# A mixture-of-experts layer pair on one core: conditional blocks between its phases replaced by one at the end, with 23 instead of 24 quads of expert tiles

## The chip, the cores and the metric

One core of a Trainium2 chip. The metric is device time in microseconds (us) of one execution; the figure for a kernel is the median of its runs.

## The reference

4,096 tokens (16 sequences of 256) of width 128 go through half an expert layer, attention, and half an expert layer again, with the same expert weights both times:

```
x = x + 0.5 * ffn(layernorm(x))
x = x + attention(layernorm(x))
x = x + 0.5 * ffn(layernorm(x))

ffn(x): t = rmsnorm(x) * norm_scale;  g = t @ gate_w.T + gate_b          # 32 experts
        vals, idx = top_k(g, 4);      w = softmax(vals)
        out = sum over the 4 experts e of w_e * (w2_e @ swiglu(w1_e @ t + b1_e) + b2_e)
        return x + out
```

Attention is linear (queries and keys are softmaxed over the width, scores are divided by their sum), 16 heads of 8. All is float32.

## The kernel before

**Tiles.** Tokens come in blocks of 512 (four subtiles of 128) and groups of four blocks; there are two groups, 0 and 1. For each group and each of the two expert layers the kernel sorts token rows by expert: in each subtile an expert's rows are rounded up to units of RB = 5, an expert's units of the whole group to tiles of BT = 25 units (125 rows of width 128). A tile belongs to one expert. Four tiles make a quad. At most NT = 112 tiles (NQ = 28 quads) can be needed, whatever the routing; how many are needed is known only on the chip.

**Phases.** `experts(st, lo, hi, beside)` (line 684) runs the quads of one group in one layer. Four such phases follow one another: first layer of group 0 and 1, last layer of group 0 and 1. Here they are called f0, f1, l0 and l1. Each runs NQS = 24 quads. In a phase, `enter(q)` loads a quad's rows from DRAM (`xq`, two DMAs on SyncE's queue, L696), lets GpSimd copy the four tiles' first weights out of `w_sb` at an address read from a table (L703), and transposes the rows on TensorE (`pxT`, L709); `first(q)` is the first matmul (`ph`, 16 instructions, L723) with its activation on ScalarE (L727) and VectorE (L728, L733); `second(q)` is the second (`po`, 8 instructions, L741), the copy out of PSUM on ScalarE (`yq`, L746) and two stores to DRAM (`ys`, L748, SyncE).

**Beside it.** After each quad `beside()` takes a few steps of another chain of work, so that TensorE has both in its queue. Beside f0 goes `enter(1)`: norm, gate and top-4 of group 1 (`route`, L437) and its sorting (`dispatch`, L519), whose end is 16 scatters of rows (`xs`, L589, GpSimd's queue; the five `p` matmuls at L665 and the copies at L669 and L670 make the rows). Beside f1 goes `middle(0)`: it gathers the results of f0 (`gt<-ys`, L784), combines them (`pa`, `pwb`, L796 to L798, then `pu`, L814 and L817), does the attention of group 0, routes its last layer and scatters. Beside l0 goes `middle(1)`, beside l1 `leave(0)` (gathers, combines, stores the output); `leave(1)` stands alone at the end. `finish()` emits what is left of a chain. So l0 needs the scatters of `middle(0)`, f1 those of `enter(1)`, l1 those of `middle(1)`; and a gather needs all stores of its phase.

**Missing tiles.** `dispatch` also writes `over`, the number of experts that end before tile NQS*NJ; it is 32 if the first NQS quads hold all tiles (L584). After f0, and again after l0, `others` takes the smaller `over` of the two groups (L763), loads it into a register of every engine (`values_load`, L764), and puts the quads 24 to 27 of both groups into a conditional block (L768), so that the program is cut there: every engine branches. On the way that leaves the quads out, each engine's semaphores are set to what the quads would have made them, and SyncE does so only after the DMAs before it have landed. At the start, zeros are written to the rows of `ys` that the first NQS quads do not write (L266).

**Order.** Each engine works through its own queue in order. The order is set when the program is built, out of the order in the code and the dependencies; within one block, instructions of different phases can be interleaved, across a block's edge they cannot.

Of the kernel before, what the change touches and what calls it, by code (L numbers as in the profile page):

```python
# [13 lines left out]
I32 = mybir.dt.int32  # L14
AF = mybir.ActivationFunctionType
ALU = mybir.AluOpType
# [6 lines left out]
P = 128  # L23
# [3 lines left out]
GB = 4  # L27
GJ = GB * NJ
NE = 32
# [13 lines left out]
NT = (GJ * P + NE * (BT - 1)) // BT  # L43
NT = -(-NT // NJ) * NJ
NQ = NT // NJ
NQS = 24
NB = NT * BT
LIMIT = 7.0
ALPHA = 1.702
# [7 lines left out]
def kernel(  # L57
# [22 lines left out]
    nc = tc.nc  # L80
    n_tok = x.shape[0]
    n_blk = n_tok // TB
    n_grp = n_blk // GB
# [9 lines left out]
    small = ctx.enter_context(tc.tile_pool(name="small", bufs=2))  # L93
# [8 lines left out]
    x_tiles = {}  # L102

    def load_x(b):
        xt = tmp.tile([P, NJ, P], F32, tag="rows", name=f"x_{b}", bufs=8)
        nc.sync.dma_start(xt.rearrange("p (i s) h -> p i (s h)", i=SEQ), x_blk[b])
        x_tiles[b] = xt
# [153 lines left out]
    for g in range(n_grp):  # L261
        rest = ys[g][NQS * NJ * BT :, :].rearrange("n w -> (n w)").rearrange(
            "(p c w) -> p c w", p=P, c=4
# [69 lines left out]
    def moments(srcs, name):  # L333

        n = len(srcs) * NJ
        bufs = 2 if len(srcs) == 1 else 1
        stats = small.tile(
            [P, n, nc.vector.BN_STATS_DIM], F32, tag=f"stats{n}", name=f"st_{name}", bufs=bufs
        )
        mv = small.tile(  # L340
            [P, n, nc.vector.BN_AGGR_DIM], F32, tag=f"mv{n}", name=f"mv_{name}", bufs=bufs
        )
        for j in range(n):
            nc.vector.bn_stats(stats[:, j, :], srcs[j // NJ][:, j % NJ, :])
            nc.vector.bn_aggr(mv[:, j, :], stats[:, j, :])
        return mv

    def inverse_root(v, y, t):

        nc.vector.tensor_scalar(  # L350
            t.bitcast(I32), v.bitcast(I32), 1, None, ALU.logical_shift_right
        )
        nc.vector.tensor_scalar(
            y.bitcast(I32), t.bitcast(I32), -1.0, float(0x5F3759DF), ALU.mult, ALU.add
        )
        for _ in range(3):
            nc.vector.scalar_tensor_tensor(t, y, -0.5, v, ALU.mult, ALU.mult)
            nc.vector.tensor_tensor(t, t, y, ALU.mult)
            nc.vector.scalar_tensor_tensor(y, t, 1.5, y, ALU.add, ALU.mult)
        return y  # L360

    def coefficients(srcs, name):

        mv = moments(srcs, name)
        mean, var = mv[:, :, 0], mv[:, :, 1]
        n = len(srcs) * NJ
        bufs = 2 if len(srcs) == 1 else 1

        def new(tag, k):
            return small.tile([P, k, n], F32, tag=f"{tag}{n}", name=f"{tag}_{name}", bufs=bufs)  # L370


        rr, it, co = new("rr", 2), new("it", 2), new("co", 4)
        ra = it[:, 0, :]
        nc.vector.tensor_scalar(rr[:, 0, :], var, EPS, None, ALU.add)
        nc.vector.reciprocal(ra, rr[:, 0, :])
        nc.vector.tensor_tensor(ra, ra, var, ALU.mult)
        nc.vector.tensor_scalar(rr[:, 1, :], ra, EPS, None, ALU.add)
        rr = inverse_root(rr, new("iy", 2), it)

        nc.vector.tensor_tensor(co[:, 0, :], rr[:, 0, :], rr[:, 1, :], ALU.mult)
        nc.vector.scalar_tensor_tensor(
            co[:, 1, :], co[:, 0, :], -1.0, mean, ALU.mult, ALU.mult
        )
        nc.vector.tensor_scalar(co[:, 2, :], rr[:, 0, :], 0.5, 1.0, ALU.mult, ALU.add)
        nc.vector.scalar_tensor_tensor(
            co[:, 3, :], rr[:, 0, :], -0.5, mean, ALU.mult, ALU.mult
        )
        return co
# [4 lines left out]
    class Group:  # L394
# [12 lines left out]
        def enter(self, b):  # L407
            self.blocks.append(Block())
            self.held(b, "tn", [P, NJ, P], F32, GB + 1)
            self.blocks[b].xr = dram.tile(  # L410
                [P, NJ * P], F32, tag=f"xr_{self.name}{b}", name=f"xr_{self.name}{b}"
            )

            self.held(b, "rank", [P, P], BF16, 2 * GB + 2)
            self.held(b, "combT", [P, P], F32, 2 * GB + 2)
            return self.blocks[b]
# [102 lines left out]
    def dispatch(st, clear=False):  # L519
# [63 lines left out]
        st.over = grp.tile([P, 1], F32, tag="over", name=f"over_{name}", bufs=4)  # L583
        nc.vector.tensor_copy(st.over, pex[:, NQS * NJ : NQS * NJ + 1])  # L584
        yield
# [98 lines left out]
    def experts(st, lo, hi, beside):  # L684
# [51 lines left out]
        def second(q):  # L736
# [10 lines left out]
            for rows in parts:  # L747
                nc.sync.dma_start(ys_q[q].rearrange("j m h -> m j h")[rows], yq[rows])  # L748

        enter(lo)  # L750
        for q in range(lo, hi + 1):
            if q + 1 < hi:
                enter(q + 1)
            if q < hi:
                first(q)
            if q > lo:
                second(q - 1)
            beside()

    def others(a, b):  # L760

        over = small.tile([P, 1], I32, tag="over", name=f"over_{a.name}{b.name}", bufs=1)
        nc.vector.tensor_tensor(over, a.over, b.over, ALU.min)  # L763
        taken = nc.values_load(  # L764
            over[0:1, 0:1], min_val=0, max_val=NE,
            skip_runtime_bounds_check_because="made on the chip, a count of experts",
        )
        with tc.If(taken < NE):  # L768
            for st in (a, b):
                experts(st, NQS, NQ, lambda: None)  # L770

    def combined(st, b, tag):

        name = f"{st.name}{b}"
# [149 lines left out]
    waiting = deque()  # L924

    def step(n=1):
        for _ in range(n):
            while waiting:
                try:
                    next(waiting[0])  # L930
                    break
                except StopIteration:
                    waiting.popleft()

    def finish():
        while waiting:
            step()

    first = [Group(g, f"f{g}") for g in range(n_grp)]
    last = {}  # L940

    def staggered(chains, gap, most=2):

        chains = deque(chains)
        going = deque()
        while chains or going:
            if chains and len(going) < most and (not going or going[-1][1] >= gap):
                going.append([chains.popleft(), 0])
            for c in list(going):
                try:  # L950
                    next(c[0])
                    c[1] += 1
                    yield
                except StopIteration:
                    going.remove(c)

    def routes(g, gap, most):
        srcs = []
        for b in range(GB):
            if g > 0:  # L960
                load_x(g * GB + b)
            srcs.append(x_tiles.pop(g * GB + b))
        co = coefficients(srcs, f"f{g}")
        yield

        def block(b):
            yield from route(first[g], srcs[b], b, co[:, :, b * NJ : (b + 1) * NJ])

        yield from staggered((block(b) for b in range(GB)), gap, most)

    def enter(g):
        yield from routes(g, 2, 2)
        yield from dispatch(first[g], True)

    def middle(g):
        last[g] = Group(g, f"l{g}")

        def block(b):
            for x1 in combined(first[g], b, "x1"):
                yield  # L980
            for x2 in attention(x1, f"{g}{b}"):
                yield
            yield from route(last[g], x2, b, coefficients([x2], f"l{g}{b}"))

        yield from staggered((block(b) for b in range(GB)), 12)
        yield from dispatch(last[g])

    def leave(g):
        def block(b):
            for y in combined(last[g], b, "x1"):  # L990
                yield
            nc.sync.dma_start(
                out_blk[g * GB + b], y.rearrange("p (i s) h -> p i (s h)", i=SEQ)
            )
            yield

        yield from staggered((block(b) for b in range(GB)), 3)
# [10 lines left out]
    b1_rows = dram.tile([NE, 2 * P], F32, tag="b1_rows", name="b1_rows")  # L1008
    nc.scalar.dma_start(b1_rows, b1_t)

    waiting.append(routes(0, 1, GB))
    for c in range(NE // 2):
        step(2)
# [27 lines left out]
    banks.clear()  # L1041
    banks.append((ps_bg, "bg"))
    fold_attention()
    beside = [enter(1), middle(0), middle(1), leave(0)]
    steps = [3, 6, 6, 2]
    for i in range(2 * n_grp):
        waiting.append(beside[i])
        experts(first[i] if i < n_grp else last[i - n_grp], 0, NQS, lambda: step(steps[i]))
        finish()
        if i % 2 == 0:  # L1050
            others(*((first if i == 0 else last)[g] for g in range(n_grp)))
    waiting.append(leave(1))
    finish()


# [59 lines left out]
```

## Time and profile before

| | |
|---|---|
| median of 3 runs | 747.09 us (746.89 to 747.17) |
| the profiled execution | 768.92 us |
| its span, first to last instruction | 767.2 us |
| mean granted TensorE clock | 0.922 |
| HBM | 58.80 MB read, 64.04 MB written |
| first TensorE work of f0, f1, l0, l1 | 87.19, 217.09, 405.78, 619.60 us |
| last work before the output's last store is issued | 763.82 us |

The profile was taken in an execution of its own, longer than the runs; sums over its rows are made against its own time. Its span is cut into rows by engine. A group line reads: source line, engine, operation, output<-inputs, shape, count | busy us, mean ns of one | idle us of the engine just before them, and what ended most of it. PE is TensorE's matmuls, PEld its weight loads, DVE VectorE, ACT ScalarE, POOL GpSimd, SP SyncE; a "q" behind an engine's name is its sequencer or its DMA queue. Names that end in `_f` or `_l` belong to the first or the last layer. In a timeline, the number in brackets is the idle time before an instruction and what ended it.

### The profile page before, as it was taken

What the parts mean: (1) busy time and instruction counts of PE and PEld (TensorE: products, weight loads), DVE (VectorE), ACT (ScalarE), POOL (GpSimd) and SP (SyncE); (2) the same over time, 40 slices, a digit from 0 to 9 for tenths busy, and PEclk for the clock granted to TensorE, in tenths of its full rate; (3) what the DMA queues carried; (4) which work ended last, traced back from release to release, by engine and by line L of the source; (5) the groups of instructions that cost most, each with busy time, mean ns of one, the idle gap of its engine ahead of it and who ended that gap; (6) DMA issues with size and microseconds to landing.
All of it is one profiled execution on the core that took longest, in us unless ns stands there. A gap on an engine that the chain in (4) does not pass through costs nothing. (4 is left out here: it accounts for less than half of the span.)

```text
span 767.2 us, 16355 instructions
## 1 busy us (share of the span) xinstructions
PE 646.2 (84%) x4995; PEld 602.6 (79%) x5009; DVE 489.8 (64%) x1833; ACT 385.8 (50%) x918; POOL 291.2 (38%) x583
## 2 busy tenths in 40 slices
PE   3877598879969998897987889888889769999776
PEld 1567588879868888896886889878878659999776
DVE  6864777755527988965763587678767436654534
ACT  2843498445517458465452547464665414545410
POOL 3024433676363432121464231321226265543152
PEclk9978799999979999997998988898989979999989
DMA  7997355665565635223446342522435466766464
GB/s 235 369 334 280 124 148 163 216 234 188 144 165 137 175 84 149 55 83 108 168 168 187 112 144 69 139 79 68 107 111 184 155 157 196 222 170 176 118 185 157
DMA packets 136924, 123.98 MB, mean 162 GB/s; under 512 B 9858, under 2 KB 123970, under 8 KB 136834
## 3 DMA queue, kind: packets, MB, share of 16 engines
q1 hardware_dynamic: 121890, 73.16, 33.8%
q0 software_dynamic: 10960, 44.90, 17.5%
q10 hardware_dynamic: 3984, 4.82, 1.8%
q8 instruction: 45, 0.74, 0.4%
q14 instruction: 45, 0.37, 0.1%
HBM read 58.80 MB, written 64.04 MB: 160 GB/s over the span
## 5 line engine op out<-in xcount | busy, mean ns | idle before, releaser
L703 POOL COPY w_l<-w_sb 128x256 f32 x192 | 72.5, 407 | 144.5 <-PE ph_l L723 124.4
L703 POOL COPY w_f<-w_sb 128x256 f32 x192 | 74.0, 417 | 121.7 <-PE ph_f L723 108.3
L723 PE MATMUL ph_f<-xT_f,w_f 128*128 128x125 f32 x768 | 104.7, 285 | 2.9 <-DVE lin_f L728 1.6
L723 PE MATMUL ph_l<-xT_l,w_l 128*128 128x125 f32 x768 | 102.5, 284 | 0.0
L723 PEld LDWEIGHTS ph_f<-xT_f,w_f 128*128 128x128 f32 x768 | 98.0, 201 | 4.8 <-POOL w_f L703 2.7
L723 PEld LDWEIGHTS ph_l<-xT_l,w_l 128*128 128x128 f32 x768 | 96.6, 200 | 1.0 <-issue 0.9
L728 DVE TENSOR_SCALAR lin_f<-ph_f 128x250 f32<-128x250 f32 x96 | 39.3, 413 | 56.5 <-ACT a_f L727 46.5
L728 DVE TENSOR_SCALAR lin_l<-ph_l 128x250 f32<-128x250 f32 x96 | 39.4, 413 | 56.1 <-ACT a_l L727 55.5
L665 PE MATMUL p_f<-tn_f,o_f 128*128 128x128 f32 x320 | 47.1, 310 | 14.6 <-ACT s_f L669 6.5
L665 PEld LDWEIGHTS p_f<-tn_f,o_f 128*128 128x128 f32 x320 | 44.3, 221 | 16.9 <-ACT s_f L669 7.2
L741 PE MATMUL po_l<-w_sb,a_l 128*125 x384 | 55.3, 288 | 2.5 <-DVE a_l L733 1.7
L741 PE MATMUL po_f<-w_sb,a_f 128*125 x384 | 53.9, 283 | 3.1 <-ACT yq_f L746 1.3
L741 PEld LDWEIGHTS po_l<-w_sb,a_l 128*125 128x125 f32 x384 | 49.8, 200 | 4.2 <-ACT yq_l L746 2.1
L727 ACT ACTIVATE a_f<-ph_f 128x250 f32<-128x250 f32 x96 | 36.3, 384 | 33.3 <-PE ph_f L723 23.2
L727 ACT ACTIVATE a_l<-ph_l 128x250 f32<-128x250 f32 x96 | 36.0, 380 | 33.7 <-PE ph_l L723 27.1
L814 PE MATMUL pu_f<-gt_f,u_f 128*128 128x128 f32 x320 | 48.5, 295 | 5.0 <-DMA gt_f<-ys,row_f 4.5
L814 PE MATMUL pu_l<-gt_l,u_l 128*128 128x128 f32 x320 | 44.0, 283 | 9.0 <-DMA gt_l<-ys,row_l 7.7
L741 PEld LDWEIGHTS po_f<-w_sb,a_f 128*125 128x125 f32 x384 | 47.9, 194 | 4.6 <-ACT yq_f L746 2.6
L814 PEld LDWEIGHTS pu_l<-gt_l,u_l 128*128 128x128 f32 x320 | 40.8, 197 | 12.1 <-issue 8.5
L784 POOL DMA_INDIRECT gt_f<-ys,row_f x32 | 32.3, 1010 | 47.1 <-PE pu_f L814 25.6
L814 PEld LDWEIGHTS pu_f<-gt_f,u_f 128*128 128x128 f32 x320 | 43.8, 208 | 6.2 <-DMA gt_f<-ys,row_f 3.5
L589 POOL DMA_INDIRECT xs<-s_f,row_f x32 | 31.1, 972 | 44.7 <-ACT s_f L670 21.6
(338 smaller groups left out, 1464.0 us busy)
## 6 DMA issues: line engine op xcount, KB each, us to landing
xq_f<-xs SPq DMA_DIRECT2D x48, 224.0 KB
ys<-yq_f SPq DMA_DIRECT2D x48, 224.0 KB
xq_l<-xs SPq DMA_DIRECT2D x48, 224.0 KB
ys<-yq_l SPq DMA_DIRECT2D x48, 224.0 KB
xs<-zero SPq DMA_DIRECT2D x14, 500.0 KB
w_sb<-in_w_dram SPq DMA_DIRECT2D x4, 1024.0 KB
x<-in_x_dram SPq DMA_DIRECT2D x8, 256.0 KB
xr_f<-xr_f ACTq DMA_DIRECT2D x8, 256.0 KB
```

The lines of the kernel that those rows point to most:

```text
L589: ins = nc.gpsimd.indirect_dma_start(out=xs[st.g][:, :], out_offset=bass.IndirectOffsetOnAxis(ap=index, axis=0), in_=rows.rearrange("p r h ...
L665: nc.tensor.matmul(p0[:, r, :] if r < 4 else p1[:, 0:P], o[:, r, :], k.tn[:, t, :], start=True, stop=True,)
L703: nc.gpsimd.tensor_copy(w[:, s, :], w_flat[:, bass.ds(at[2 * c + s], 2 * P)])
L723: nc.tensor.matmul(ph[:, part, s, 0:RT], w_q[c][:, s, part * P : (part + 1) * P], x_q[:, 2 * c + s, :], start=True, stop=True,)
L727: nc.scalar.activation(a[:, ts, :], ph[:, 0, :, 0:RT], AF.Silu, scale=ALPHA)
L728: nc.vector.tensor_scalar(lin[:, ts, :], ph[:, 1, :, 0:RT], LIMIT + 1.0, 1.0 - LIMIT, ALU.min, ALU.max,)
L741: nc.tensor.matmul(po[:RT, t, :], hT[:, t, :], w_flat[:, bass.ds(at[t] + 2 * P, P)], start=True, stop=True,)
L784: nc.gpsimd.indirect_dma_start(out=gt.rearrange("p r h -> p (r h)"), out_offset=None, in_=ys[st.g][:, :], in_offset=bass.IndirectOffsetOnA ...
L814: nc.tensor.matmul(pu[:, t, :], u[:, r, s, :], got[t][:, r, :], start=(r == 0), stop=False)
```

## The change

NQS goes from 24 to 23, so that a phase covers 92 tiles instead of 96. `others` and its two conditional blocks are gone; the four phases stand in one block. The four phases and their side chains are put into a function `groups(nq, clear)`. After its first call, `over` of all four sorts is reduced to the smallest, loaded once, and one conditional block repeats everything from the input rows on with NQ = 28 quads per phase. `Group` objects are made when a chain begins, the input of group 0 is loaded again in the repetition, and tiles and DRAM buffers of the repetition get names of their own. The program grows from about 9,700 instructions to about 19,000, of which 9,926 stand in the conditional block; of these, 4,329 are TensorE's and 740 SyncE's. In the program before, a conditional block holds 195 of TensorE's, 57 of ScalarE's and 49 to 52 of SyncE's.

```diff
-NQS = 24
+NQS = 23
...
-    def others(a, b):
-
-        over = small.tile([P, 1], I32, tag="over", name=f"over_{a.name}{b.name}", bufs=1)
-        nc.vector.tensor_tensor(over, a.over, b.over, ALU.min)
-        taken = nc.values_load(
-            over[0:1, 0:1], min_val=0, max_val=NE,
-            skip_runtime_bounds_check_because="made on the chip, a count of experts",
-        )
-        with tc.If(taken < NE):
-            for st in (a, b):
-                experts(st, NQS, NQ, lambda: None)
...
-    first = [Group(g, f"f{g}") for g in range(n_grp)]
-    last = {}
+    first, last = {}, {}
+    run_name = ""
...
-            if g > 0:
+            if g * GB + b not in x_tiles:
                 load_x(g * GB + b)
...
-    def enter(g):
+    def enter(g, clear):
+        first[g] = Group(g, f"{run_name}f{g}")
         yield from routes(g, 2, 2)
-        yield from dispatch(first[g], True)
+        yield from dispatch(first[g], clear)
...
-    beside = [enter(1), middle(0), middle(1), leave(0)]
-    steps = [3, 6, 6, 2]
-    for i in range(2 * n_grp):
-        waiting.append(beside[i])
-        experts(first[i] if i < n_grp else last[i - n_grp], 0, NQS, lambda: step(steps[i]))
-        finish()
-        if i % 2 == 0:
-            others(*((first if i == 0 else last)[g] for g in range(n_grp)))
-    waiting.append(leave(1))
-    finish()
+
+    def groups(nq, clear):
+
+
+        beside = [enter(1, clear), middle(0), middle(1), leave(0)]
+        steps = [3, 6, 6, 2]
+        for i in range(2 * n_grp):
+            waiting.append(beside[i])
+            st = first[i] if i < n_grp else last[i - n_grp]
+            experts(st, 0, nq, lambda: step(steps[i]))
+            finish()
+        waiting.append(leave(1))
+        finish()
+
+    groups(NQS, True)
+
+    over = small.tile([P, 1], I32, tag="most", name="most", bufs=1)
+    for st in (first[1], *last.values()):
+        nc.vector.tensor_tensor(first[0].over, first[0].over, st.over, ALU.min)
+    nc.vector.tensor_copy(over, first[0].over)
+    taken = nc.values_load(
+        over[0:1, 0:1], min_val=0, max_val=NE,
+        skip_runtime_bounds_check_because="made on the chip, a count of experts",
+    )
+    with tc.If(taken < NE):
+        run_name = "r"
+        waiting.append(enter(0, False))
+        finish()
+        groups(NQ, False)
```

More of the change, by code (lines that the diff above doesn't have):

```diff
@@ L959, in routes @@
         for b in range(GB):
-            if g > 0:
+            if g * GB + b not in x_tiles:
                 load_x(g * GB + b)
             srcs.append(x_tiles.pop(g * GB + b))
-        co = coefficients(srcs, f"f{g}")
+        co = coefficients(srcs, first[g].name)
         yield
@@ L969, in routes @@
         yield from staggered((block(b) for b in range(GB)), gap, most)
-    def enter(g):
+    def enter(g, clear):
+        first[g] = Group(g, f"{run_name}f{g}")
         yield from routes(g, 2, 2)
-        yield from dispatch(first[g], True)
+        yield from dispatch(first[g], clear)
     def middle(g):
-        last[g] = Group(g, f"l{g}")
+        last[g] = Group(g, f"{run_name}l{g}")
         def block(b):
@@ L980, in block @@
                 yield
-            for x2 in attention(x1, f"{g}{b}"):
+            for x2 in attention(x1, f"{run_name}{g}{b}"):
                 yield
-            yield from route(last[g], x2, b, coefficients([x2], f"l{g}{b}"))
+            yield from route(last[g], x2, b, coefficients([x2], f"{last[g].name}{b}"))
         yield from staggered((block(b) for b in range(GB)), 12)
@@ L1009 @@
     nc.scalar.dma_start(b1_rows, b1_t)
+    first[0] = Group(0, "f0")
     waiting.append(routes(0, 1, GB))
```

## The prediction

> **What bounds it now.** I read the page, then windows by stage, then the timeline where phases meet (f0, f1, l0, l1 are the four phases).
>
> ```profile
> PE 646.2 (84%) x4995; PEld 602.6 (79%) x5009; DVE 489.8 (64%) x1833; ACT 385.8 (50%) x918; POOL 291.2 (38%) x583
> ...
> L703 POOL COPY w_f<-w_sb 128x256 f32 x192 | 74.0, 417 | 121.7 <-PE ph_f L723 108.3
> ```
>
> TensorE (PE) carries the kernel. 192 copies are 2 groups x 24 quads x 4 tiles, so the conditional blocks ran none of their quads. They cost time all the same. Windows before and across each change of phase (stretch, length, busy us of PE, PEld, DVE, ACT, POOL, granted clock, DMA share, GB/s):
>
> ```profile
> 195.00:205.00 10.00, 10.00 (x93) 10.00 (x93) 4.94 (x10) 5.77 (x13) 3.10 (x11) 1.00 0.53 143
> 205.00:227.00 22.00, 13.77 (x90) 12.35 (x90) 7.92 (x19) 5.02 (x10) 10.32 (x19) 0.77 0.55 143
> 396.00:406.00 10.00, 7.33 (x62) 6.82 (x61) 2.61 (x5) 4.10 (x10) 5.29 (x11) 1.00 0.58 196
> 406.00:424.00 18.00, 14.59 (x95) 13.66 (x95) 6.68 (x17) 3.97 (x9) 10.43 (x16) 0.81 0.66 189
> 612.00:628.00 16.00, 7.72 (x40) 6.47 (x39) 5.30 (x14) 3.08 (x7) 8.91 (x18) 0.68 0.64 162
> ```
>
> PE is full in f0's last quads, idle 8.2 us around the first block (205 to 227) and 8.3 around the second (612 to 628). Around f1 to l0, where no block stands, it idles 2.7 + 3.4 us: a part of each gap is the data, not the block. The first gap in the timeline (start, us):
>
> ```profile
> 208.54 1.11 PE L741 MATMUL po_f<-w_sb,a_f 128*125 x8 [0.85 <-DVE a_f L733]
> 209.92 1.02 PE L798 MATMUL pwb_f<-comb_f,seg_f 128*128 128x512 f32 x2
> 214.05 15.15 SPq L696 DMA_DIRECT2D xq_f<-xs  x10
> 214.69 1.00 POOL L784 DMA_INDIRECT gt_f<-ys,row_f  x1 [13.52 <-SPq L768]
> 217.09 1.06 PE L709 MATMUL pxT_f<-ident,xq_f 125*128 125x125 f32 x4 [6.15 <-DMA xq_f<-xs]
> 219.33 1.19 PE L814 MATMUL pu_f<-gt_f,u_f 128*128 128x128 f32 x4 [1.17 <-DMA gt_f<-ys,row_f]
> ```
>
> SP may not load f1's first rows before the block's exit (it waits there for the stores in flight), though f1's last scatter was issued at 191.1. The second gap, and the branch itself:
>
> ```profile
> 599.12 6.46 PE L665 MATMUL p_l<-tn_l,o_l 128*128 128x128 f32 x40 [2.39 <-DVE o_l L657]
> 607.14 1.08 POOL L589 DMA_INDIRECT xs<-s_l,row_l  x1 [0.80 <-DVE lin_l L728]
> 616.27 11.73 SPq L696 DMA_DIRECT2D xq_l<-xs  x10
> 619.60 1.07 PE L709 MATMUL pxT_l<-ident,xq_l 125*128 125x125 f32 x4 [6.97 <-DMA xq_l<-xs]
> ```
>
> ```profile
> L768 PEldq COMPARE_BRANCH  x2: 3462/3808/4153, 209.5 to 611.2; - x2
> L768 ACTq COMPARE_BRANCH  x2: 45/45/45, 212.1 to 613.2; - x2
> L768 SPq COMPARE_BRANCH  x2: 50/50/50, 212.7 to 615.0; - x2
> ```
>
> **Is the repetition taken?** The new test at the end repeats everything if any of four groups needs over 92 tiles. That is data. I routed the reference's own inputs with the reference's top-4, split each block into its four subtiles, rounded each expert's count up to 5 and its rows up to 25: 90 and 87 tiles in f0 and f1, 90 and 87 in l0 and l1. Two tiles of margin; a tie decided otherwise moves a row, not three tiles. So the repetition should not run, and I go on with that.
>
> **The change part by part** (against the profiled 768.92; minus is a gain).
>
> 1. The 24th quad in f0 and l1. The last quads there start every 3.09 us (pxT at 707.47, 710.56) with PE full: 16 ph, 8 po and 4 pxT matmuls back to back. Nothing else sets the pace, enter(1) and leave(0) being done. 2 x 3.09 = -6.2.
>
> 2. The first block. In the changed program's order PE goes from f0's last po straight to f1's pxT, whose rows SP now loads among f0's last quads. But ys still has to land before the first gather gt, and PE takes its queue in order: after pxT, pwb, pxT, 8 ph, 4 ph, pxT, 4 ph and half a po it meets pu. I count that as 6.6 us at the full clock from the last po's end (8 ph 0.9, 8 po 0.9, 4 pxT 0.43, pwb 1.3). The chain yq copy 0.6, stores 1.3 behind one load on SP, landing 2.5 (ys at the end of the chain of waits) and gather to pu 4.6 (214.69 to 219.33) is 9.2. So pu stalls 2.6 and starts at +9.2, where before it started at +9.7 (209.65 to 219.33). By then the new order has done 4.9 us more of work (2 pxT, 16 ph, half a po). 0.5 + 4.9 = -5.3. Behind pu in PE's queue stand f1's next quads, so these 2.6 are real.
> [...] Between 0 and 2.3 I take -1.0. Part 2: -6.3 (ends -3 and -9).
>
> 3. f1 to l0. No block goes, but a quad does. Before, PE's order is: the last 20 p_l, 2 ph, a quad's po, the 24th quad's 16 ph, two quads' po, then pxT_l at 405.78, 8.0 us after the last p_l (397.76). That wait is the scatter, its landing, and SP's load, so the removed quad lay under it; ahead of the last p_l the changed order has only 0.2 us less. What is late next is the load itself. Its second half now stands behind the two stores of the last yq on SP (0.45 us each): pxT_l at about +9.1. Against that, the last stores go 2.5 us earlier, the gathers too, and pu starts near +14.1 instead of +17.9 (415.70), with 2.2 us less of work behind it. 3.8 - 2.2 = 1.6, less about 1 for a longer slow-clock stretch: -0.6 (ends +2 and -3.1, the whole quad).
>
> 4. l0 to l1, block two. The last p_l ends at 605.58; pxT_l came 14.0 after it. Without the block the same path as in 3: +9.1. That is -4.9, and the quad is in it (it lies under the same path). POOL's w copies and gathers are no longer held (7.5 us, released by PE's branch), so nothing new is late. Ends -2.5 and -8.
>
> 5. More zeros. ys's tail grows from 16 to 20 tiles: 2 x 0.25 MB at the start. DMA is full there (356 GB/s in 50 to 60) and the scatters of f0 wait on landing (4.1 us before 65.58): 0.5 MB / 356 = +1.4 (ends 0 and +1.5).
>
> 6. The new ending. Four small DVE minima and a copy (0.15 each) hide under PE. Then every engine loads the value (0.43 to 1.04 at L764) and branches over the whole repeated program. [...] The rows agree by engine: ACT and SP jumped some 50 instructions in 0.05 us, PE 195 in 3.5 to 4.2. Now SP jumps 740, PE 4,329. By ACT's row the end costs about +0.8 (eight waits, another hop); by PE's, SP, which issues the last output at 764.2, arrives at 764.2 + 0.55 + 3.8 = 768.6, past the present end of 767.2, and leaves about 1.1 later: +2.5. I take the latter (ends +0.8 and +4.5).
>
> Sum: -6.2 - 6.3 - 0.6 - 4.9 + 1.4 + 2.5 = -14.1, to 754.8 in the profile. The unprofiled median is 747.09/768.92 = 0.972 of the profiled time: -13.7, so **733.4**.
>
> **Rivals.**
> - *Gain at the joins is mostly given back* (17%). PE's in-order queue meets pu and pxT_l as at f1 to l0, and the blocks only hid those waits. For: that join idles 6.1 us without any block. Against: f1's rows are ready from about 194. Then parts 2 and 4 give -2 each: -6.2 - 4 + 1.4 + 2.5 = -6.3, or 741.
> - *All of it* (16%). Short stalls keep the clock up, the zeros hide, the branch is cheap: -6.2 - 9 - 3.1 - 8 + 0.8 = -25.5, or 722.
> - *The repetition runs* (2%): one group with a 93rd tile decides it. The price is a second pass with 28 quads per phase, without the weight loading before 87: about 733 + 0.97 x (680 + 20 x 3.09) = 1,450. Slower by far; the tile counts speak against it.
> - *The end alone eats the gain* (2%): would need over 16 us in part 6, four times PE's longest branch.
>
> The sum's case has 63%. 0.2% is 1.5 us, about what a measurement can tell from none. Range 726 to 741: it takes in the sum with its ends, not added all on one side, and reaches the first rival; left out are the outer part of the second, and the repetition. The ends together would give 722 to 744. Faster 95%, same 1%, slower 4%.
>
> **What would show it.** 184 copies per w tile, none more. PE idle between f0's last po and f1's first pxT under 1 us, then a stall of 2 to 3 before the first pu, with a lower clock or not. pxT_l after the last p_l of about 9 us at both later joins. The f0 phase beginning 1 to 1.5 us later than 87.19. Long branches on all engines at the end, and 2 to 3 us from the last output's issue more than now. It is wrong if the joins wait for something not counted here (SP's order of loads and stores, above all), or if a phase's inner pace changes with the new order.

## The result, and the profile after

The changed kernel took **737.72 us** (median of 6 runs, 736.46 to 746.78), the kernel before beside it 747.92 (6 runs, 746.89 to 750.70): 0.9876 of the time, with a 95% interval of 0.9840 to 0.9912. The forecast was 733.4 with a range of 726 to 741; the interval allows a gain of 0.9% to 1.6%.

The 768.92 us of the profile that the prediction is built on was an unusually long execution. A second profile of the same kernel took 749.91 us (span 748.2), and the comparison below is made with that one. TensorE did its work in the same order in both; the first had a lower granted clock (0.922 against 0.936).

What to look at first is time by phase, not the two totals. Each row is a stretch from one phase's first `pxT` to the next one's: the start with the weight loading, f0, f1, l0, l1, and the rest. The columns are stretch, length, busy us of PE, PEld, DVE, ACT and POOL, granted clock, DMA share, GB/s. First the kernel before, in its second profile:

```profile
0.00:87.00 87.00, 53.59 (x308) 40.05 (x309) 58.97 (x307) 37.55 (x99) 26.95 (x70) 0.90 0.86 289
87.00:209.30 122.30, 109.14 (x948) 105.15 (x948) 81.91 (x264) 78.63 (x178) 61.24 (x125) 0.96 0.61 182
209.30:396.00 186.70, 166.54 (x1332) 158.06 (x1332) 134.76 (x542) 104.46 (x255) 71.17 (x140) 0.94 0.44 132
396.00:599.00 203.00, 171.95 (x1339) 160.64 (x1340) 144.32 (x565) 108.05 (x259) 69.45 (x130) 0.93 0.43 128
599.00:704.40 105.40, 103.06 (x877) 99.95 (x878) 51.56 (x109) 50.58 (x114) 47.16 (x104) 0.97 0.66 180
704.40:748.20 43.80, 30.79 (x208) 27.00 (x206) 18.36 (x47) 5.38 (x13) 15.12 (x16) 0.88 0.52 160
```

The same windows of the changed kernel:

```profile
0.00:87.70 87.70, 55.87 (x307) 41.60 (x307) 58.79 (x306) 37.62 (x99) 26.49 (x70) 0.88 0.88 292
87.70:202.90 115.20, 106.60 (x917) 103.32 (x918) 75.88 (x251) 75.94 (x172) 62.80 (x125) 0.96 0.61 185
202.90:398.40 195.50, 166.53 (x1314) 154.59 (x1313) 142.33 (x562) 106.51 (x256) 67.69 (x130) 0.96 0.43 128
398.40:585.90 187.50, 164.75 (x1308) 155.47 (x1308) 137.04 (x552) 103.30 (x252) 66.98 (x128) 0.93 0.45 133
585.90:688.20 102.30, 100.13 (x849) 97.29 (x850) 50.06 (x106) 48.82 (x110) 45.90 (x98) 0.97 0.64 180
688.20:734.70 46.50, 30.82 (x208) 27.04 (x206) 18.37 (x47) 5.38 (x13) 15.14 (x16) 0.87 0.50 153
```

The prediction's six parts can be put on the same stretches. Part 2's -6.3 is -7.4 in f0 (the wait before `pxT` goes) and +1.1 in f1 (the wait at `pu` and its clock). Part 3's -0.6 is +1.1 in f1 (`pxT_l` later) and -1.7 in l0.

| stretch | predicted | measured |
|---|---|---|
| start | +1.4 | +0.7 |
| f0 | -3.1 - 7.4 = -10.5 | -7.1 |
| f1 | +1.1 + 1.1 = +2.2 | **+8.8** |
| l0 | -1.7 - 4.9 = -6.6 | **-15.5** |
| l1 | -3.1 | -3.1 |
| rest | +2.5 | +2.7 |
| sum | -14.1 | -13.5 |

The sum agrees with these two profiles, but three stretches do not: f1 lost 6.6 us more than forecast, f0 gained 3.4 less, and l0 gained 8.9 more. A total that fits because errors cancel explains nothing yet. The two profiles also differ by more than the medians do (13.5 against 10.2 us): the changed kernel's was the quickest of its six runs, 736.46 us.

At the joins themselves the forecast can be read in the timeline (start and length in us, engine, line, operation, count, and in brackets the idle time before it and who ended it). From f0 to f1, first the kernel before in its second profile:

```profile
201.01 1.11 PE L741 MATMUL po_f<-w_sb,a_f 128*125 x8 [0.85 <-DVE a_f L733]
...
209.34 1.06 PE L709 MATMUL pxT_f<-ident,xq_f 125*128 125x125 f32 x4 [5.92 <-DMA xq_f<-xs]
211.66 1.19 PE L814 MATMUL pu_f<-gt_f,u_f 128*128 128x128 f32 x4 [1.26 <-DMA gt_f<-ys,row_f]
```

and the changed kernel:

```profile
202.88 0.59 PE L709 MATMUL pxT_f<-ident,xq_f 125*128 125x125 f32 x4
203.31 0.38 PE L784 MATMUL pa_f<-rank_cf,seg_b_f 128*128 128x512 bf16 x1
...
209.69 0.60 PE L741 MATMUL po_f<-w_sb,a_f 128*125 x4
212.62 1.38 PE L802 MATMUL pu_f<-gt_f,u_f 128*128 128x128 f32 x10 [2.33 <-DMA gt_f<-ys,row_f]
213.84 0.56 PE L805 MATMUL pu_f<-b_sb,comb_f 128*128 128x128 f32 x2
214.20 2.34 PE L802 MATMUL pu_f<-gt_f,u_f 128*128 128x128 f32 x10
```

PE goes from `po` to `pxT` without idling and stands 2.33 us at the first `pu` (forecast 2.6), which starts 9.6 us after f0's last `po` ends (forecast 9.2). The second ten `pu` behind that wait take 2.34 us (granted clock 0.50 from 213.9 to 217.3); at a granted clock of 1.00 ten take 1.28 (at 218.81). From l0 to l1:

```profile
571.18 5.02 PE L665 MATMUL p_l<-tn_l,o_l 128*128 128x128 f32 x40
...
585.88 1.06 PE L709 MATMUL pxT_l<-ident,xq_l 125*128 125x125 f32 x4 [5.35 <-DMA xq_l<-xs]
```

`pxT_l` comes 9.7 us after the last `p_l` (571.18 + 5.02) at this join, and 9.75 at f1 to l0; the forecast said 9.1 for both. Before, in the second profile, these were 13.3 and 8.8.

### The profile page after: what moved, and what is told of

It is laid out like the page before. It is cut to its first block, busy times and chain, and to the rows that moved or that the text cites. A ratio compares the mean times of both kernels' runs of the same rounds, so it can differ in the third digit from the quotient of the medians.

```text
span 734.7 us, 15957 instructions
## 1 busy us (share of the span) xinstructions
PE 624.7 (85%) x4897; PEld 579.3 (79%) x4897; DVE 482.5 (66%) x1823; ACT 377.6 (51%) x902; POOL 285.0 (39%) x567
## 5 line engine op out<-in xcount | busy, mean ns | idle before, releaser
L703 POOL COPY w_f<-w_sb 128x256 f32 x184 | 71.5, 420 | 129.4 <-PE ph_f L723 120.5
L703 POOL COPY w_l<-w_sb 128x256 f32 x184 | 68.7, 404 | 120.3 <-PE ph_l L723 108.7
L723 PE MATMUL ph_f<-xT_f,w_f 128*128 128x125 f32 x736 | 98.6, 282 | 1.5 <-DVE lin_f L728 1.3
L723 PE MATMUL ph_l<-xT_l,w_l 128*128 128x125 f32 x736 | 99.6, 286 | 0.2 <-DVE mv_a L838 0.2
L723 PEld LDWEIGHTS ph_l<-xT_l,w_l 128*128 128x128 f32 x736 | 93.9, 202 | 1.4 <-issue 1.3
L723 PEld LDWEIGHTS ph_f<-xT_f,w_f 128*128 128x128 f32 x736 | 91.8, 198 | 2.8 <-issue 2.1
L741 PE MATMUL po_l<-w_sb,a_l 128*125 x368 | 51.4, 282 | 2.8 <-ACT yq_l L746 1.0
L772 POOL DMA_INDIRECT gt_l<-ys,row_l x32 | 30.6, 957 | 50.5 <-PE pu_l L802 23.7
L741 PEld LDWEIGHTS po_l<-w_sb,a_l 128*125 128x125 f32 x368 | 45.9, 194 | 4.0 <-ACT yq_l L746 2.2
L802 PE MATMUL pu_f<-gt_f,u_f 128*128 128x128 f32 x320 | 45.8, 284 | 2.8 <-DMA gt_f<-ys,row_f 2.3
```

The lines of the kernel that those rows point to most:

```text
L703: nc.gpsimd.tensor_copy(w[:, s, :], w_flat[:, bass.ds(at[2 * c + s], 2 * P)])
L723: nc.tensor.matmul(ph[:, part, s, 0:RT], w_q[c][:, s, part * P : (part + 1) * P], x_q[:, 2 * c + s, :], start=True, stop=True,)
L741: nc.tensor.matmul(po[:RT, t, :], hT[:, t, :], w_flat[:, bass.ds(at[t] + 2 * P, P)], start=True, stop=True,)
L772: nc.gpsimd.indirect_dma_start(out=gt.rearrange("p r h -> p (r h)"), out_offset=None, in_=ys[st.g][:, :], in_offset=bass.IndirectOffsetOnA ...
L802: nc.tensor.matmul(pu[:, t, :], u[:, r, s, :], got[t][:, r, :], start=(r == 0), stop=False)
```

## Experiments

Each kernel ran beside the kernel before, whose medians in these comparisons were 749.2 to 751.9 us. All profiles are single executions. One program instruction can be two rows of a trace: block 0's 24 `pu` are 48 rows.

**How far apart are two executions?** The kernel before, unchanged, compared with itself.

> The kernel before, unchanged, for a second trace. The first trace took 768.92 us where its runs take about 748, and its phase l0 is 214 us long where the changed kernel's is 190. If the first trace was an odd execution, l0 is about 190 here too and the span near 746. If the change itself shortened l0, it is 214 again. Either way the ratio is 1.000.

749.98 us, ratio 1.0014 (0.9985 to 1.0042). Its 20 runs go from 742.74 to 754.78. So a median tells some 0.3%, a single profile much less. Three kernels below that share one order in f1 (the changed one, the one without the ending, the one with l0 by hand) have f1 at 195.5, 195.3 and 197.1 us, so differences of 2 us between single profiles say nothing. The first profile of the kernel before, with its lower clock, has l0 at 213.8 where the second has 203.0.

**Only fewer quads.**

```diff
-NQS = 24
+NQS = 23
```

> The kernel before with 23 quads, the two blocks kept: quads and zeros alone. My sum: the quads of f0 and l1 count (-6.2), those of f1 and l0 lie under the path from the last p matmuls to the next phase's rows (-0.6 and 0), zeros +1.4: about -5 us, 743, ratio 0.993. The rival that a quad is worth its 3.09 us of TensorE in every phase: -11 us, 737, ratio 0.985. If the blocks hide the quads: no change.

734.26 us, ratio 0.9833 (0.9782 to 0.9883): with both blocks still there, at least as fast as the whole change, and near the 737 of the rival that this expectation names. But not by its account: l1 lost 2.6 us in the profile, while l0 lost 14.7 (203.0 to 188.3), against a quad's 3.1.

**Only no blocks** (the tiles beyond 96 would be left out; there are none with these inputs).

```diff
-        if i % 2 == 0:
-            others(*((first if i == 0 else last)[g] for g in range(n_grp)))
```

> The kernel before with 24 quads and no conditional block anywhere (it leaves out the tiles past the 96th, of which there are none here). The blocks alone, without the new ending. My sum: -6.3 at f0 to f1 and -4.9 at l0 to l1, x 0.97 = -11, 737, ratio 0.985. The rival that the joins only change their wait: -2 each, 744, ratio 0.995.

753.67 us, ratio 1.0108 (1.0051 to 1.0165): **slower**. Yet f0 fell by 5.3 us (7.4 were foreseen for its join) and l0 by 5.0 (4.9 foreseen). f1 rose from 186.7 to 199.1.

**No ending** (the repetition for an overfull choice is left out).

```diff
-    with tc.If(taken < NE):
-        run_name = "r"
-        waiting.append(enter(0, False))
-        finish()
-        groups(NQ, False)
```

> The changed kernel without the conditional block at the end (it leaves out the repetition, which is not needed here). My sum: 2.5 us less than the changed kernel, with the span ending about 3.4 us after the last vector instruction instead of 6.2: ratio to before about 0.984. The rival that the branches hide under the last output's landing: the same time as the changed kernel, 0.9876.

736.77 us, ratio 0.9858 (0.9806 to 0.9910). From the last store's issue to the end it takes 3.3 us (728.0 to 731.3), in the changed kernel 6.2 (728.5 to 734.7), before 3.4: part 6 is +2.9, forecast +2.5. The medians, 0.95 us apart and taken in different comparisons, cannot show it. f1 is 195.3 and l0 187.4, so the ending has nothing to do with those.

By now the joins and the end are near the forecast, and what moves the time is the pace inside f1 and l0. There the build had written TensorE's queue in one of two orders. They differ in where the work beside the experts stands. In the **wide** order the four transposes of attention's normed input (`ph<-h`) stand in quad 5; in the **tight** one in quad 4. In both, block 0's 24 `pu`, whose result the norm reads, end in quad 2, so the tight order leaves the norm on VectorE less time: between the last of these `pu` and the first `ph` PE has some 4.9 us of other matmuls in the tight order and 6.5 in the wide one (from the changed kernel's f1, 220.3 to 225.2, and from f1 by hand below, 224.8 to 231.3). The theory: the order makes the pace. The rival: f1 is longer because nothing drains f0's stores and gathers ahead of it.

**A step taken ahead.** Three attempts to get the wide order by an edit of the schedule: in the changed kernel for i == 1, in the kernel before for i == 2, and without blocks with 24 quads for both.

```diff
         waiting.append(beside[i])
+        if i == 1:
+            step(1)
```

> The changed kernel, whole, with one step of the work beside it taken ahead of the expert tiles of f1 (and of no other phase). In the program's order the weights' product pwb of block 0's combine then stands before f1's first pxT, and its 24 pu stand together before the last of quad 1's ph; l0 is as in the changed kernel. Theory A (f1 lost 9 to 12 us because its queue on TensorE was written in another order: pwb between the first two pxT and the pu behind quad 1's ph): f1 falls from 195.5 to about 185 us and the time from 737 to about 727 us. Theory B (f1 is longer because the gathers and the writes of f0, which the block used to drain, now run into it, whatever the order): f1 stays at 194 to 196 us and the time at 737 us.

> The kernel before, with 24 quads and both blocks, and one step of the work beside it taken ahead of the expert tiles of l0 alone. In the program's order l0's pwb then stands before its first pxT and the pu stand together, as in the quick phases; f0, f1 and l1 are untouched. Theory A (order): l0 falls from 203 to about 190 us and the time by 10 to 14 us, to about 736 us, though no quad and no block is gone. Theory B (l0 became quick since a quad of its work or of the one before went): l0 stays at 203 us and the time at 748 us.

> The kernel before with 24 quads, without the two blocks (so the tiles of an overfull choice would be left out; there are none here), and with one step of the work beside it taken ahead of f1's and of l0's expert tiles. The same without that step took 753.7 us, 1.1% more than the kernel before, with 199 us in f1 and 198 in l0. Theory A (order): f1 falls to about 186 and l0 to about 186 us, the time to about 730 us: the joins' 10 us are then seen in the time. Theory B (joins without blocks leave the next phase slower by themselves): both stay within 3 us of 199 and 198 and the time at 750 us or more.

734.92 us (0.9814, 0.9782 to 0.9846), 742.11 (0.9904, 0.9871 to 0.9937) and 745.90 (0.9944, 0.9902 to 0.9986). The expected 727, 736 and 730 were missed: f1 stayed at 193.6 us in the first, l0 at 195.8 in the second, and the third had 195.6 and 194.4. The build had made a third order, with the 24 `pu` together, but the transposes still in quad 4. So setting `pwb` and `pu` ahead, which these expectations took for the mark, does not give the quick phase. It is not worth nothing either: the medians are 2.8, 7.4 and 7.8 us below those of the same kernels without the step (the first and the third pair ran in different comparisons). The first of the three, read alone, spoke for the rival.

**24 quads in the changed kernel.**

```diff
-NQS = 23
+NQS = 24
```

> The changed kernel with 24 quads of expert tiles per phase again, all else as it is. In the program's order f1 and l0 then both have pwb between the first two pxT and the pu behind quad 1's ph. Theory A (order): l0 loses what the changed kernel gained there, 10 to 12 us, beside 6 us for the two quads of f0 and l1: about 755 us, slower than the kernel before. Theory B (the quads alone, 3.1 us in f0 and in l1 each and something in l0): about 744 us.

755.10 us, ratio 1.0066 (1.0037 to 1.0094), as the theory said: l0 went to the tight order and to 200.7 us.

**The order by hand.** This parts the theory from the rival. The 751 matmuls and transposes of a phase are chained in a given order, and nothing else is edited; in the traces PE's order in the phase is then the one asked for. "Quads 0 to 13" is the stretch from the start of quad 0's `pxT` to the start of quad 13's.

```diff
+            n0 = len(nc.cur_bb.bb.instructions)
             experts(st, 0, nq, lambda: step(steps[i]))
             finish()
+            if clear and i == 1:
+                ordered(nc.cur_bb.bb.instructions[n0:])
...
+        for a, b in zip(at, at[1:]):
+            tc.add_manual_dep(mm[b], mm[a].name, info, reason="order")
```

> The changed kernel, whole, without blocks, with one thing done by hand: the 751 matmuls and transposes that TensorE does in f1 stand in exactly the order that they have in the kernel with blocks and 23 quads (its f1 took 185.3 us). Nothing is added or taken away; in all other phases the order is the changed kernel's own. Theory A (order: f1 lost its time because the matmuls of the work beside the experts stand a quad nearer to what they wait for): f1 falls from 195.5 to 185 to 188 us, quads 0 to 13 from 94 to about 83 us, and the time to about 727 us. Theory B (without the block before it, f1 is longer whatever the order, since f0's last writes and the first gathers run into it): quads 0 to 13 stay at 94 us or more and the time at 737 us.

732.62 us, ratio 0.9746 (0.9712 to 0.9779), faster than either kernel. Quads 0 to 13 of f1 took 87.3 us where they took 94.4; the expected 83 was missed, mainly by one wait. PE's waits in f1's quads 0 to 13 (who waited <- for what, us in total, times, longest), changed kernel:

```profile
PE pt_l L285 <- DVE tn_l L444: 4.3, 2, 2.8
PE ph L285 <- DVE h L844: 3.6, 2, 2.1
PE pu_f L802 <- DMA gt_f<-ys,row_f: 2.3, 1, 2.3
```

and with the order by hand:

```profile
PE pu_f L802 <- DMA gt_f<-ys,row_f: 6.3, 1, 6.3
PE pt_l L285 <- DVE tn_l L444: 1.6, 2, 1.3
PE prank_l L480 <- DVE m_l L471: 1.3, 1, 1.3
PE ph L285 <- DVE h L844: 1.1, 1, 1.1
```

The waits for VectorE's norms (`h`, `tn_l`) fall from 7.9 to 2.7 us. What stood behind the longer of these waits also ran slower. In the changed kernel eight `plog_k` take 1.87 us, behind a wait of 2.06 us (granted clock 0.51 from 227.5 to 230.9):

```profile
227.24 0.70 PE L285 MATMUL ph<-ident,h 128*128 128x128 f32 x2 [2.06 <-DVE h L844]
...
229.46 1.87 PE L815 MATMUL plog_k<-wk_sb,hT 128*128 128x128 f32 x8 [0.26 <-ACT hT L851]
```

and with the order by hand 1.11, behind a wait of 1.12 us:

```profile
232.45 0.33 PE L285 MATMUL ph<-ident,h 128*128 128x128 f32 x1 [1.12 <-DVE h L844]
...
234.27 1.11 PE L815 MATMUL plog_k<-wk_sb,hT 128*128 128x128 f32 x8
```

Behind the changed kernel's two waits for `tn_l` in the same stretch the granted clock was 0.52 (252 to 255, after 2.84 us) and 1.00 (282.3 to 286, after 1.41 us).

But the wide order has two `pu` (four rows) at its very head; with a block ahead they had waited 0.8 us for their gathers, and here PE waits 6.3 us. So the rival had a part of it: in quads 0 to 13 some 4 of the 11.5 us, in this order. Over the whole phase it is more: f1 went from 195.5 to 192.1 us, where the kernel with blocks has 185.3, so that only 3.4 of 10.2 us came back. (Quads 0 to 13 hold ten rows of PE more in the tight order, 618 against 608, which is a part of the difference.) The median fell by 5.1 us.

> The changed kernel, whole, with the matmuls and transposes of TensorE in l0 put by hand in the order that the changed kernel has in f1 (the two phases consist of the same 751 of them); f1 itself is left as it is. Theory A (order): quads 0 to 13 of l0 go from 82.8 to about 95 us, as in the kernel before, l0 from 187.5 to about 199 us, and the time from 737 to about 748 us, no faster than the kernel before. Theory B (l0 became quick for another reason, such as the quad less): l0 stays within 3 us of 187.5 us and the time at 737 us.

754.31 us, ratio 1.0025 (1.0000 to 1.0049): the tight order put into l0 alone takes the whole gain away. Quads 0 to 13 of l0 went from 82.8 to 98.3 us, l0 to 201.1. The waits there are those of f1 again:

```profile
PE pt_l L285 <- DVE tn_l L444: 4.9, 2, 3.4
PE ph L285 <- DVE h L844: 3.8, 2, 2.3
```

> The kernel before with 23 quads and both blocks, with the matmuls and transposes of TensorE in f1 put by hand in the order that the changed kernel has there. The same without that took 734.3 us, f1 in it 185.3 us. Theory A (order): quads 0 to 13 of f1 go from 82 to about 94 us although the block stands ahead of them, and the time to about 745 us. Theory B (the block ahead of f1 is what makes it quick): f1 stays at 185 us and the time at 734 us.

The edit is the same chain, in the kernel with both blocks and 23 quads. 743.65 us, ratio 0.9880 (0.9844 to 0.9916), against 0.9833 without it: a block right ahead of f1 does not make it quick. Quads 0 to 13 took 95.6 us instead of 82.0.

**The wide order without its early `pu`.** The table of the run above, with the first 18 `pu` set behind quad 0's `po`:

```diff
-    ORDER = [(16, 3), (0, 4), (19, 2), (4, 12), (21, 38), ...
+    ORDER = [(16, 3), (0, 16), (37, 16), (19, 18), (53, 6), ...
```

> The changed kernel, whole, with f1's matmuls in the order of the kernel with blocks, but for the first 18 pu of block 0's combine: they stand behind quad 0's po, in front of the last 6 pu, and no longer between quads 0 and 1. In the run with the unaltered order TensorE stood 6.3 us at the first of them, waiting for the gathers of f0's last results (with a block ahead of f1 that wait was 0.8 us), so that f1 took 192.1 and not 185 us and the time was 732.6 us. Theory A (what was left of f1's loss is this one wait): about 5 us more of expert work stands in front of it, the wait falls to 1 to 2 us, quads 0 to 13 from 87.3 to 83 us, f1 to about 187 us and the time to about 728 us. Theory B (the wait only moves on, since x1's norm behind the pu then comes late for the transposes in quad 5): f1 stays at about 192 us and the time at 732 us.

732.36 us, ratio 0.9754 (0.9715 to 0.9794), no better than the order unaltered. In the profile the wait for the gathers is gone as expected:

```profile
PE pu_f L802 <- DMA gt_f<-ys,row_f: 1.0, 1, 1.0
```

and f1 is 187.5 us against 192.1. But that execution, 722.38 us, was the quickest of the six (the median is ten above it), l0 had come out in yet another order there (180.8 us), and the two kernels ran in different comparisons. What moving the `pu` is worth stays open.

All phases side by side, in us: first quads 0 to 13, then the whole phase. T is the tight order, W the wide one, O another; in brackets is the quad of the first `h` transposes.

| kernel | block ahead of f1 | f1 | l0 |
|---|---|---|---|
| before, second profile | yes | W (5) 82.9, 186.6 | T (4) 95.8, 203.0 |
| 23 quads, blocks kept | yes | W (5) 82.0, 185.3 | W (5) 82.5, 188.3 |
| no blocks, 24 quads | no | T (4) 96.9, 199.1 | T (4) 98.6, 198.0 |
| **changed** | no | **T (4) 94.4, 195.5** | **W (5) 82.8, 187.5** |
| no ending | no | T (4) 94.4, 195.3 | W (5) 82.3, 187.4 |
| changed, 24 quads | no | T (4) 94.1, 194.3 | T (4) 98.6, 200.7 |
| step ahead in f1 | no | O (4) 100.1, 193.6 | W (5) 82.7, 187.6 |
| before, step ahead in l0 | yes | W (5) 80.8, 180.7 | O (4) 98.4, 195.8 |
| no blocks, steps ahead | no | O (4) 96.5, 195.6 | O (4) 101.8, 194.4 |
| f1 by hand | no | W (5) 87.3, 192.1 | W (5) 82.5, 185.7 |
| l0 by hand | no | T (4) 96.1, 197.1 | T (4) 98.3, 201.1 |
| blocks, f1 by hand | yes | T (4) 95.6, 199.3 | O (5) 80.0, 184.8 |
| f1 by hand, `pu` later | no | O (5) 82.7, 187.5 | O (5) 80.3, 180.8 |

In all 26 phases one mark goes with the pace. With the transposes of `h` in quad 5 the whole phase takes 180.7 to 192.1 us, in quad 4 193.6 to 203.0. Quads 0 to 13 divide the same way (80 to 87, and 94 to 102), but there the four O (4) phases are not like the rest: their stretch holds 638 to 678 rows of PE, where the tight order has 613 to 618 and the others 604 to 608. The orders made by hand show that PE's order sets the pace. They move many matmuls at once, so which of them matters is not shown; the place of `h` is a mark, which no run moved alone.

## Why the prediction was right, and where it was not

The time fell inside the range, but by luck: two large errors of opposite sign met. It is 4.3 us above the forecast and 3.3 below the first rival's 741, so no nearer to the likeliest case than to that rival. Point by point:

1. *The 24th quad* (-6.2). In l1 it is -3.1, to the tenth. In f0 the quad's 3.1 us are gone as well, but quads 15 and 16 took 16.4 us instead of 12.7, so that quads 0 to 22 took 3.2 us longer. No run tests this stretch by itself, but it goes with the number of quads: the two take 15.1 to 17.5 us in the eight kernels with 23 quads, with and without blocks, and 12.1 to 15.1 in those with 24. Why stays open.
2. *The first block* (-6.3). The start of `pu` (+9.6 for +9.2), its stall (2.33 for 2.6) and the slow matmuls behind it are near what was worked out. The 6.6 us of work ahead of `pu` took 7.2; it comes out of the stated costs only with 32 rows of `ph`, which the timeline has (20 and 12), not with 16. The -1.0 for the clock, between 0 and 2.3, was an estimate, and no run shows that term. What the traces show is the granted clock behind two such waits. In the first profile of the kernel before it was 0.50 from 415.7 to 421.5, behind a wait of 3.31 us, and ten `pu` took 2.50 us:

```profile
415.70 2.50 PE L814 MATMUL pu_f<-gt_f,u_f 128*128 128x128 f32 x10 [3.31 <-DMA gt_f<-ys,row_f]
```

In the changed kernel the wait of 2.33 us was also followed by 0.50; the second rival's short stalls, which keep the clock up, were not seen at this join. At that clock PE then worked for 3.4 us in f1's head (213.9 to 217.3), where it had worked 5.4 us so before (217.1 to 223.7 in the first profile, the idle time taken off); an estimate from these two, half their difference, is a saving of 1.0 us.
3. *f1 to l0* (-0.6). `pxT_l` came 9.75 us after the last `p_l`, forecast 9.1. The part's "about 1 for a longer slow-clock stretch" was an estimate, and the traces show no longer one: at a granted clock of 0.50 PE worked 5.9 us before (415.7 to 421.6 in the first profile) and 6.0 in the changed kernel (398.4 to 405.0). What l0 gained beyond this is not in this part at all.
4. *The second block* (-4.9). 9.7 for 9.1, and 13.3 before: -3.6.
5. *The zeros* (+1.4). In one profile +0.7. Over all profiles f0 begins at 86.1 to 87.4 us with 24 quads and at 87.6 to 89.4 with 23: about +1.8 on the means, and near the forecast.
6. *The ending* (+2.5). +2.9. PE's branch is hidden, as worked out, and SP is what ends late. But the time does not stand where I put it. Line 1058 is the new test (instruction, count, shortest/median/longest in ns, first and last start):

```profile
L1058 PEldq COMPARE_BRANCH  x1: 3340/3340/3340, 726.4 to 726.4; - x1
L1058 SPq COMPARE_BRANCH  x1: 45/45/45, 729.5 to 729.5; - x1
L1058 SPq EVENT_SEMAPHORE  x8: 17/17/17, 732.1 to 732.6; - x8
```

SP's branch takes 0.045 us, not 3.8; its next instruction comes 2.6 us after it. The size was hit with the wrong row as its ground.

**The step that failed** is the silent one under parts 1 to 4: that each phase keeps its inner pace, so that only quads and joins count. The text named it at its end ("a phase's inner pace changes with the new order") and gave it no price. It was the largest term. With the first block gone the build put f1 into the tight order; with a quad gone it put l0 into the wide one. Against the forecast f1 is +6.6 and l0 -8.9, f0, mostly in its quads 15 and 16, is +3.4, and together these nearly cancelled. The two halves of the change, each alone, show the size: 1.7% faster with fewer quads, 1.1% slower without blocks.

So the joins' gain is real and did not reach the total: at f0 to f1 it is spent again within f1. In the tight order PE waits for VectorE's norms, and works at half pace behind those of 2.06 and 2.84 us (granted clock 0.51 and 0.52 in the changed kernel's f1; busy 81.4 us in quads 0 to 13, 75.3 by hand in the wide order; an estimated 1 us of that is the ten rows more); in the wide order without a block it waits for the gathers. The 23 quads alone, with the blocks kept, have the whole of the measured gain, and most of theirs is l0's order: put back into the tight one, the changed kernel takes 754.31 us.

The first rival, gain given back at the joins, would have given 741: the right account for f1, by another mechanism (not the join's waits, but order).

The factor 0.972 from the profiled to the measured time was worked from one long execution; for the second profile the two agree within 2 us, and profiling did not lengthen that one.

## What to carry to other kernels

When an edit changes where blocks begin or how many steps a phase has, compare the built order of the bound engine before and after, phase by phase, before any sum is made; here a group of transposes one quad nearer to its producer went with a loss larger than what the edit saved at the join. A barrier's price is not its gap alone: here it also let data land that the next phase's first instructions would wait for (0.8 us of waiting at the first `pu` with a block ahead, 6.3 without). A total that fits is checked stretch by stretch.

## What the runs showed of the hardware

- One kernel's executions spread by more than 10 us, and the granted clock goes with it: of the 20 runs of the kernel before, the two at 0.949 and 0.952 took 742.74 and 744.73 us, the one at 0.930 took 753.30.
- The jump over the repeated program cost every engine 2.5 to 3.4 us, but in different places. PE's branch row itself lasts 3.34 us. The rows of the others last 0.05 to 0.07 us, and the next instruction comes late: ACT goes on after 2.5 us (717.5 to 720.0), SP and POOL after 2.6, DVE after 3.2. In the kernel before, over some 50 instructions, ACT went on after 0.4 us (204.6 to 205.0) and SP after 0.5 (205.1 to 205.6). So for these two the longer jump cost 2.1 us more; where that time goes the traces do not show. PE's branch took 3.5 to 4.2 us over 195 instructions, no less than over 4,329, so its price did not grow with the distance.
